# Windowed attention and a gated low-rank feed-forward: the gated factors carried in the block moves, the feed-forward product in two parts, value differences from SBUF, queries normed in place

## The chip, the cores and the metric

One Trainium2 chip, one of its cores. The metric is the device time of one execution in microseconds. Everything is float32.

## The reference, cut to what matters

There are 32 sequences of 512 tokens of 256 features, 16 query heads and 4 key heads of 64 features, a window of 128 tokens, and a feed-forward with 8 gated low-rank parts of rank 16.

```python
x = x + attn(layernorm(x)); x = x + ffn(layernorm(x))

def attn(x, wq, wk, wv, wo, q_norm_w, k_norm_w):
    q, k, v = rmsnorm(x @ wq.T, q_norm_w), rmsnorm(x @ wk.T, k_norm_w), x @ wv.T   # per head
    scores = q k^T / 8, kept where (i >= j) & (i - j < 128)
    return (softmax(scores) @ v) @ wo.T

def ffn(x, weight, gate_w, lora_U, lora_V):
    gate = softmax(x @ gate_w.T)                       # 8 gates
    base = x @ weight.T
    t = einsum('nh,erh->ner', x, lora_U)               # 8 x 16 factors
    lora = einsum('ne,eor,ner->no', gate, lora_V, t)
    return base + lora / 16
```

## The kernel before, in words

The work is cut into 128 tiles of 128 tokens, four to a sequence (`t` = 0 to 3). A tile passes through a pipeline of small steps. `slot(i)` writes out one turn of the pipeline: it names, in order, which step is issued for which tile, so while tile `i` has its inputs transposed (`trx`), tile `i-3` has its scores made (`s_pe`), tile `i-6` its values summed (`y_pe`), tile `i-7` its output product (`o_pe`), tile `i-10` its feed-forward product (`f_pe`), and tile `i-11` is stored. The order within each engine is exactly the order of this list; nothing is reordered later. The first 12 turns are in a table `FIRST`, the last ones in `LAST`, and `slot(i)` runs for i = 12 to 127. `BANK` and `PLACES` fix which of four single PSUM banks (B0 to B3) a product goes to; the scores have two double banks (S0, S1) of their own, each used twice in a turn.

What each step does, with its engine and line:

- TensorE (PE): `kv_pe` L398 and `q_pe` L413 are the key, value and query products (two chunks of 128 features, 512 columns each; a float32 product is two instructions, so four per 512 columns). `s_pe` L529 makes scores for 32 queries of a head pair against 160 keys. `y_pe` L627 multiplies probabilities and values in 16 half-width instructions, then, for `t` > 0, adds a correction in 16 quarter-size ones. `o_pe` L654 is the output product, 16 instructions of 256 columns. `f_pe` L700 multiplies the normed hidden rows by 392 columns at once: 128 of lora_U, 8 of the gate and 256 of the base weight, into one bank `f`. `uT_pe` L731 transposes the gated factors `u`, one instruction of 128 columns. `lora_pe` L738 adds lora onto the base columns that still lie in the bank `f`.
- ScalarE (ACT): copies and squares of k, v and q out of PSUM (L404, L408, L421, L426), `q_eps` L441, the exponentials `exps` L556 (16 per tile, each with an accumulator read), `y_copy` L648, `kT_copy` L511, `hT_copy` L690, `uT_copy` L735, `gexp` L714, and `ln1_neg` L385, which makes minus the row scale for `vdiff`.
- VectorE (DVE): sums of squares (`qsum` L435), the score merge and maximum (`s_merge` L540, `nmaxs` L545), transposes of 32x32 blocks (`tr`, `trk`, `trq`, `trh`, `trx`), `vdiff` L613 and L616 (the difference between a tile's values and the values of the tile before), `o_add`, `gmax`, `gmul` L720, `store` L745.
- GpSimd (POOL): all powers (`pow` L319 for the norms of q and k, and the two layer-norm scales), `kn` and `qn` (keys and queries times their norms), `prob` L568 (exponentials times the reciprocal of their sum), `pick` L599 (masks for the correction in `y_pe`).
- SyncE (SP): DMA issues. A transpose on VectorE only turns 32x32 blocks; the blocks are then sent to their places by `move`, 16 DMAs per tile. What must be transposed is written into one buffer `tr` (`blocks_of(n)`) in pieces: queries (0 to KO), keys (KO to PO), probabilities (PO to HO) and hidden rows (HO on), each of another tile; `move(n)` sends all of them to a buffer `pT` (`moved[n]`), and consumers read their piece. SP also loads x in two layouts and stores the result (`put` L750).

In `vdiff` one operand is the value product in PSUM, the other a tile in SBUF:

```python
nc.vector.scalar_tensor_tensor(
    self.vd[lo], own[lo], self.ln1.rs[lo], old[lo], ALU.mult, ALU.subtract
)
```

Of the kernel before, what the change touches and what calls it, by code (L numbers as in the profile page):

```python
# [8 lines left out]
F32 = mybir.dt.float32  # L9
# [5 lines left out]
P = 128  # L15
D = 256
# [14 lines left out]
def tile_window_attn_lora_ffn(  # L31
# [43 lines left out]

    nc = tc.nc
# [11 lines left out]
    XBUFS = 12  # L88
# [5 lines left out]
    DH = 4  # L94
    KO = NCH * BL
    PO = KO + GP * BL
    HO = PO + NB * 2 * GP * BL
    PIECE = HO + ND * BL
# [9 lines left out]
    for tag, products in {  # L108
        "B0": "tq0 y1 uT",
        "B1": "cqa q0 tq1 y0 o",  # L110
        "B2": "ckv cqb hT tk kv q1",
        "B3": "cf f",
        "S0": "s0 s2",
        "S1": "s1 s3",
    }.items():
        BANK.update(dict.fromkeys(products.split(), tag))
# [3 lines left out]
        ("ckv", 0): "B3",  # L120
        ("cqa", 0): "B2",
        ("cqb", 0): "B0",
        ("q0", 0): "B2",
        ("kv", 0): "B1",
        ("q0", 1): "B3",
        ("q1", 0): "B3",
        ("q0", 2): "B0",
        ("kv", 1): "B0",
        ("cf", 0): "B1",
        ("tq0", 0): "B2",  # L130
        ("tk", 0): "B3",
        ("kv", 2): "B3",
        ("tk", 1): "B0",
        ("tq0", 1): "B3",
        ("tq1", 1): "B3",
        ("q0", 3): "B0",
        ("kv", 3): "B1",
        ("tq0", 2): "B1",
        ("tq1", 2): "B2",
        ("tk", 2): "B1",  # L140
        ("q1", 4): "B0",
        ("q0", 5): "B0",
        ("kv", 5): "B3",
        ("kv", 6): "B0",
        ("y0", 0): "B0",
        ("y1", 0): "B3",
        ("q1", 6): "B3",
        ("y0", 1): "B0",
        ("y1", 1): "B3",
        ("o", 0): "B3",  # L150
        ("o", 1): "B0",
        ("y0", 2): "B3",
        ("y0", 3): "B0",
        ("y1", 3): "B3",
        ("o", 2): "B3",
        ("f", 0): "B0",
        ("y1", 4): "B3",
        ("o", 3): "B0",
        ("uT", 0): "B1",
        ("y1", 5): "B2",  # L160
        ("o", 4): "B3",
        ("y0", -6): "B2",
        ("o", -7): "B0",
        ("y0", -5): "B0",
        ("y1", -5): "B2",
        ("f", -8): "B1",
        ("y0", -4): "B0",
        ("y1", -4): "B2",
        ("o", -4): "B3",
        ("f", -7): "B2",  # L170
        ("y0", -3): "B0",
        ("y1", -3): "B3",
        ("hT", -4): "B0",
        ("y0", -2): "B2",
        ("y1", -2): "B1",
        ("uT", -6): "B1",
        ("o", -2): "B2",
        ("hT", -3): "B0",
        ("f", -5): "B1",
        ("y0", -1): "B2",  # L180
        ("y1", -1): "B3",
        ("uT", -5): "B2",
        ("o", -1): "B0",
        ("f", -4): "B0",
        ("uT", -4): "B1",
        ("uT", -3): "B1",
        ("f", -2): "B0",
        ("uT", -2): "B3",
        ("f", -1): "B2",
        ("uT", -1): "B1",  # L190
    }
    def bank(what, name, i):
# [10 lines left out]
        "qn": 2,  # L203
        "ex": 3,
        "yT": 3,
        "h": 5,
        "hT": 2,
        "u": 2,
        "uT": 2,
        "res": 2,  # L210
        "xT": 3,
        "vd": 7,
# [3 lines left out]
        "kv": 8,  # L216
# [128 lines left out]
    def move(n):  # L345
        if not EARLY - DELTA <= n < N:
            return
        lo = 0 if n + DELTA < N else PO
        hi = PIECE if n >= DH else HO if n >= 0 else PO
        moved[n] = buf("pT", [P, NB, PIECE], str(n))  # L350
        for b in range(NB):
            for c in range(NB):
                nc.sync.dma_start(  # L353
                    moved[n][b * BL : (b + 1) * BL, c, lo:hi],
                    blocks[n][c * BL : (c + 1) * BL, b, lo:hi],
                )

    class Tile:
# [22 lines left out]

        def ln1_neg(self):
            if self.t > 0:
                self.minus_rs = small.tile([P, 1], F32, tag="minus_rs", bufs=8, name=f"minus_rs_{self.n}")
                nc.scalar.activation(self.minus_rs, self.ln1.rs, AF.Copy, scale=-1.0)  # L385
# [70 lines left out]
        def qn(self):  # L456
            self.q_n = buf("qn", [P, QD], self.n)
# [148 lines left out]
        def vdiff(self):  # L606

            if self.t == 0:
                return
            self.vd = buf("vd", [P, KD], self.n)  # L610
            own, old = self.ps["kv"][:, KD:], tiles[self.i - 1].kv[:, KD:]
            lo, hi = slice(0, H), slice(H, P)
            nc.vector.scalar_tensor_tensor(  # L613
                self.vd[lo], own[lo], self.ln1.rs[lo], old[lo], ALU.mult, ALU.subtract
            )
            nc.vector.scalar_tensor_tensor(  # L616
                self.vd[hi], own[hi], self.minus_rs[hi], old[hi], ALU.mult, ALU.add
            )
# [53 lines left out]
        def trh(self):  # L672
            nc.vector.transpose(
                blocks_of(self.i + DH)[:, :, HO:].rearrange("p b (c t) -> p c b t", c=ND),
# [10 lines left out]
        def hT_copy(self):  # L685
# [3 lines left out]
            else:  # L689
                nc.scalar.copy(  # L690
                    self.hT.rearrange("p c (j t) -> p c j t", t=BL),
                    moved[self.i + DH][:, :, HO:].rearrange("p j (c t) -> p c j t", c=ND),
# [4 lines left out]
        def f_pe(self):  # L697
            ps = self.bank("f")
            for c in range(ND):
                nc.tensor.matmul(  # L700
                    ps[:, : UG + D], self.hT[:, c, :], wf_sb[:, c, :],
                    start=(c == 0), stop=(c == ND - 1),
                )

        def gmax(self):
            self.lg = small.tile([P, E], F32, tag="lg", name=f"lg_{self.n}")
            nc.vector.tensor_scalar(self.lg, self.ps["f"][:, ER:UG], self.ln2.rs, None, ALU.mult)
# [8 lines left out]
        def gmul(self):  # L716
# [5 lines left out]
                self.ps["f"][:, :ER].rearrange("p (e r) -> p e r", r=R),  # L722
# [9 lines left out]

        def uT_copy(self):
            self.uT = buf("uT", [P, P], self.n)
            nc.scalar.copy(self.uT, self.ps["uT"][:, :P])  # L735

        def lora_pe(self):
            nc.tensor.matmul(  # L738
                self.ps["f"][:, UG : UG + D], self.uT, wv_sb, start=False, stop=True,
# [3 lines left out]
        def store(self):  # L743
            self.res = buf("res", [P, D], self.n)
            nc.vector.scalar_tensor_tensor(  # L745
                self.res, self.ps["f"][:, UG : UG + D], self.ln2.rs, self.h, ALU.mult, ALU.add
# [21 lines left out]
    def slot(i):  # L768
        at(i).ln1_stats()
        at(i - 1).q_pe(0)  # L770
        at(i - 11).uT_copy()
        at(i).trx()
        at(i - 4).tr(0)
        at(i).ln1_eps()
        at(i - 1).q_copy(1)
        at(i - 4).tr(1)
        at(i).ln1_rs()
        at(i - 11).lora_pe()
        at(i - 1).qsq(1)
        at(i - 4).prob_den(1)  # L780
        at(i - 3).s_pe(0)
        at(i - 8).ln2_stats()
        at(i).ln1_neg()
        at(i - 4).prob(1)
        at(i - 11).store()
        at(i - 1).q_copy(0)
        at(i - 3).s_pe(1)
        at(i - 11).put()
        at(i - 1).qsq(0)
        at(i - 3).s_merge(0)  # L790
        at(i).kv_pe()
        at(i - 3).nmaxs(0)
        at(i - 8).ln2_eps()
        at(i - 1).qsum()
        at(i - 6).pick(1)
        at(i - 10).f_pe()
        at(i - 3).s_merge(1)
        at(i - 3).nmaxs(1)
        at(i).kv_copy()
        at(i - 8).ln2_rs()  # L800
        at(i - 4).tr(2)
        at(i).ksq()
        at(i - 6).y_pe()
        at(i - 1).q_eps()
        at(i - 3).exps(0)
        at(i).ksum()
        at(i - 1).pow()
        at(i).vdiff()
        at(i - 3).exps(1)
        at(i - 4).tr(3)  # L810
        at(i - 10).gmax()
        at(i - 3).s_pe(2)
        at(i - 6).y_copy(0)
        at(i - 3).s_pe(3)
        at(i - 3).prob_den(0)
        at(i - 6).y_copy(1)
        at(i - 3).s_merge(2)
        at(i - 7).o_pe()
        at(i - 10).gexp()
        at(i - 3).nmaxs(2)  # L820
        at(i - 1).kn()
        at(i - 3).s_merge(3)
        at(i - 1).qn()
        at(i - 1).trk()
        at(i - 3).nmaxs(3)
        at(i - 2).kT_copy()
        at(i - 10).gmul()
        at(i - 3).exps(2)
        at(i - 3).prob(0)
        at(i - 1).trq()  # L830
        at(i - 10).uT_pe()
        at(i).q_pe(1)
        at(i - 3).exps(3)
        at(i - 7).o_add()
        at(i - 5).pick(0)
        move(i - 4)
        at(i - 7).trh()
        at(i - 9).hT_copy()
# [5 lines left out]
        ldb:2 ldb:3 mean_kv:0 ldx:0 ln1_stats:0 ldb:0 ldb:1 mean_qa:0 ldx:1 ldx:3 mean_qb:0 sub_kv:0  # L844
        trx:0 ldx:5 ln1_eps:0 trx:1 sub_qa:0 ln1_rs:0 kv_pe:0 kv_copy:0 q_pe.0:0 sub_qb:0 ksq:0
        qsq.0:0 ldwo:0 q_copy.0:0 ln1_stats:1 ksum:0 ldx:4 ldx:2 ln1_eps:1 ln1_stats:2 ln1_stats:4
        q_pe.1:0 kv_pe:1 ln1_eps:2 ln1_rs:1 trx:2 ln1_neg:0 ldb:4 ldx:6 ln1_rs:2 q_pe.1:1 ln1_eps:4
        ln1_stats:3 qsq.1:0 ln1_eps:3 q_copy.1:0 qsum:0 kv_copy:1 vdiff:0 ln1_neg:1 ln1_rs:3 ldb:7
        q_pe.0:1 q_eps:0 ldwf:0 ksq:1 q_copy.1:1 vdiff:1 ldb:5 ln1_rs:4 ln1_stats:5 ldx:8 pow:0
        ldx:9 qsq.1:1 ksum:1 q_pe.0:2 ln1_stats:6 qsq.0:1 ln1_stats:8 kn:0 q_copy.0:1 mean_f:0  # L850
        ln1_eps:5 qsq.0:2 ldb:6 ln1_neg:2 qn:0 tk_pe:0 ln1_neg:4 qsum:1 sub_f:0 trx:3 q_pe.1:2
        q_eps:1 kT_copy:0 q_copy.0:2 pow:1 ln1_stats:9 tq_pe.1:0 ldx:7 ln1_neg:3 kn:1 q_copy.1:2
        kv_pe:2 ln1_eps:8 qsq.1:2 tq_copy.1:0 tq_pe.0:0 ln1_eps:6 kv_copy:2 qn:1 kv_pe:3 ksq:2
        ln1_stats:7 tk_pe:1 tq_copy.0:0 kv_copy:3 ksum:2 s_pe.1:0 qsum:2 s_pe.0:0 q_pe.1:3 ln1_rs:5
        s_merge.1:0 nmaxs.1:0 kT_copy:1 s_merge.0:0 trx:4 ksq:3 q_eps:2 ln1_rs:6 q_pe.0:3 pow:2
        exps.1:0 nmaxs.0:0 exps.0:0 vdiff:2 vdiff:3 ksum:3 qsq.1:3 q_copy.1:3 q_copy.0:3 qsq.0:3
        kn:2 tq_pe.0:1 prob_den.0:0 trx:5 tq_copy.0:1 s_pe.3:0 s_merge.3:0 prob.0:0 nmaxs.3:0 trx:6
# [152 lines left out]
```

## Time and profile before

| | |
|---|---|
| time, median of 3 runs | 2090.65 us (2089.69 to 2091.2) |
| the profiled execution's own time | 2090.21 us |
| its span, first to last instruction | 2088.5 us |
| busy share of the span | PE 99%, DVE 85%, POOL 80%, ACT 73% |
| granted TensorE clock | 1.00 |
| busy share of the 16 DMA engines | about 60% |
| four turns (one sequence) in the middle of the program | 64.24 us, of which PE is busy 64.14, DVE 55.59, POOL 52.16, ACT 47.63 |

In the timeline of one engine a line merges instructions of one kind: when the first starts, how long until the last ends, engine, line, operation, what is written and read, the shape, and how many. PE starts one matmul before the last has ended, so a group's first column minus that of the group before is what the earlier group cost; the second column is longer than that. A weight load (PEld) runs beside the matmul before it.

### The profile page before, as it was taken

Reading aid. Unit: us, or ns where it says so; the run is one execution under the profiler, and the core shown is the slowest. Engines: PE = TensorE matmul, PEld = TensorE weight load, DVE = VectorE, ACT = ScalarE, POOL = GpSimd, SP = SyncE. Lnnn points to the kernel's source line nnn. Section 1 sums busy time; section 2 is a strip of 40 time slices with the busy share of each in tenths; the row PEclk is TensorE's granted clock in tenths of the full one; section 3 lists DMA queues with packets and bytes.
Section 4 is the critical chain, followed back from the end, with each engine's and each line's share of the span. In section 5 each row is a group of like instructions: output and inputs, shape, how many; then the busy total and the mean of one; then the engine's idle time right before and its main releaser. Section 6 shows DMA issues by size and latency. Waiting matters only on the chain.

```text
span 2088.5 us, 43160 instructions
## 1 busy us (share of the span) xinstructions
PE 2071.2 (99%) x12214; PEld 1282.8 (61%) x12214; DVE 1778.1 (85%) x4546; ACT 1530.5 (73%) x6247; POOL 1670.9 (80%) x1291
## 2 busy tenths in 40 slices
PE   8999999999999999999999999999999999999999
PEld 4556666666666666666666666666666666666665
DVE  6988888888888888888888888888898888888884
ACT  6877777777777777777777777777777777777773
POOL 6988778877788788888877887778878888887773
PEclk9999999999999999999999999999999999999999
DMA  5665666566656666665666656665656566656653
GB/s 116 143 154 137 140 144 143 132 140 143 144 133 142 141 140 138 142 144 137 137 142 140 146 134 140 142 146 132 143 136 148 132 143 144 139 135 140 142 130 86
DMA packets 272989, 288.79 MB, mean 138 GB/s; under 512 B 172273, under 2 KB 206705, under 8 KB 272753
## 3 DMA queue, kind: packets, MB, share of 16 engines
q1 hardware_dynamic: 272208, 284.47, 59.6%
q8 instruction: 100, 1.64, 0.4%
q10 hardware_dynamic: 544, 1.57, 0.2%
q14 instruction: 137, 1.11, 0.2%
HBM read 36.71 MB, written 16.78 MB: 26 GB/s over the span
## 4 chain that ended last, share of the span: by engine, by line
PE 89%; ACT 6%; SPq 2%; DVE 1%; DMA 1%; issue 0%; DVEq 0%; ACTq 0%
PE o_ps L654 22%; PE q_ps L413 20%; PE s_ps L529 14%; PE y_ps L627 13%; PE kv_ps L398 11%; PE f_ps L700 6%; ACT ex L556 4%; PE f_ps L738 3%; SPq L353 1%; ACT kv L404 1%; PE uT_ps L731 1%; ACT ksq L408 1%; SPq L238 0%; DVE nmax L545 0%; DMA pT<-tr 0%
## 5 line engine op out<-in xcount | busy, mean ns | idle before, releaser
L556 ACT ACTIVATE ex<-s_ps,nmax 128x128 f32<-128x128 f32 x2048 | 720.5, 387 | 28.5 <-DVE nmax L545 22.3
L319 POOL TENSOR_TENSOR rs<-ss_eps,minus_half 128x20 f32<-128x20 f32 x128 | 453.1, 3539 | 167.1 <-ACT ss_eps L441 165.8
L568 POOL TENSOR_TENSOR ex<-ex,rden 128x1024 f32<-128x1024 f32 x256 | 485.4, 1896 | 96.8 <-DVE rden L564 95.3
L654 PE MATMUL o_ps<-wo_sb,yT 128*128 128x256 f32 x2048 | 475.3, 385 | 0.3 <-ACT yT L648 0.3
L556 ACT ACTIVATION_READ_ACCUMULATOR ex<-s_ps,nmax 128x1 f32 x2048 | 465.9, 228 | 0.0
L413 PE MATMUL q_ps<-wq_sb,xT 128*128 128x512 f32 x1024 | 462.6, 593 | 0.1
L654 PEld LDWEIGHTS o_ps<-wo_sb,yT 128*128 128x128 f32 x2048 | 379.1, 190 | 68.8 <-ACT yT L648 10.6
L545 DVE TENSOR_REDUCE nmax<-s_ps 128x4 f32<-128x512 f32 x512 | 348.6, 681 | 13.0
L529 PE MATMUL s_ps<-kT,pT 64*128 64x160 f32 (+4 forms) x4000 | 335.4, 304 | 3.9 <-ACT ex L556 0.9
L529 PEld LDWEIGHTS s_ps<-kT,pT 64*128 64x128 f32 x4000 | 271.1, 186 | 104.5 <-ACT ex L556 47.0
L599 POOL TENSOR_SCALAR_AFFINE_SELECT other<-pT 64x512 f32<-64x512 f32 x384 | 289.8, 755 | 21.3 <-DMA pT<-tr 5.9
L413 PEld LDWEIGHTS q_ps<-wq_sb,xT 128*128 128x128 f32 x1024 | 184.5, 190 | 192.2 <-issue 173.8
L404 ACT ACTIVATE kv<-kv_ps,ln_rs_a 128x512 f32<-128x512 f32 x128 | 88.3, 690 | 265.0 <-PE kv_ps L398 265.0
L398 PE MATMUL kv_ps<-wkv_sb,xT 128*128 128x512 f32 x512 | 253.5, 617 | 0.6 <-DVE xT L390 0.5
L627 PE MATMUL y_ps<-pT,kv 128*64 128x256 f32 x2048 | 249.3, 385 | 0.0
L458 POOL TENSOR_TENSOR qn<-q,rs 128x1024 f32<-128x1024 f32 x128 | 243.4, 1902 | 0.2
L579 DVE STREAM_TRANSPOSE tr<-ex 128x512 f32<-128x512 f32 (+3 forms) x512 | 240.3, 487 | 2.8 <-DMA pT<-tr 1.1
L421 ACT ACTIVATE q<-q_ps,ln_rs_a 128x512 f32<-128x512 f32 x256 | 176.0, 688 | 51.5 <-PE q_ps L413 50.3
L627 PEld LDWEIGHTS y_ps<-pT,kv 128*64 128x64 f32 x2048 | 135.5, 136 | 125.9 <-ACT ss_eps L441 61.4
L540 DVE COPY_PREDICATED s_ps<-over,s_ps 128x128 f32<-128x128 int32 x512 | 148.4, 290 | 75.4 <-PE s_ps L529 70.8
L700 PE MATMUL f_ps<-wf_sb,hT 128*128 128x392 f32 x512 | 190.1, 494 | 0.1
L426 ACT ACTIVATE qsq<-q_ps,ln_rs_a 128x512 f32<-128x512 f32 x256 | 175.0, 684 | 2.0 <-PE q_ps L413 1.2
(85 smaller groups left out, 2538.3 us busy)
## 6 DMA issues: line engine op xcount, KB each, us to landing
pT<-tr SPq DMA_DIRECT2D x1936, 112.0 KB, 2.3
xb<-in_x_dram SPq DMA_DIRECT2D x256, 64.0 KB, 2.3
x<-in_x_dram SPq DMA_DIRECT2D x128, 128.0 KB, 2.4
out_dram<-res SPq DMA_DIRECT2D x128, 128.0 KB, 2.0
pT<-tr SPq DMA_DIRECT2D x64, 104.0 KB, 2.2
pT<-tr SPq DMA_DIRECT2D x48, 72.0 KB, 2.1
wq_sb<-in_wq_dram ACTq DMA_DIRECT2D x1, 1024.0 KB, 7.4
wo_sb<-in_wo_dram SPq DMA_DIRECT2D x1, 1024.0 KB, 6.5
```

The lines of the kernel that those rows point to most:

```text
L319: nc.gpsimd.tensor_tensor(o, v, minus_half[:, : o.shape[-1]], ALU.pow)
L398: nc.tensor.matmul(ps, self.xT[:, c, :], wkv_sb[:, c, :], start=(c == 0), stop=(c == ND - 1))
L413: nc.tensor.matmul(ps, self.xT[:, c, :], wq_sb[:, c, gp * 512 : (gp + 1) * 512], start=(c == 0), stop=(c == ND - 1),)
L458: nc.gpsimd.tensor_tensor(self.q_n.rearrange("p (g d) -> p g d", d=HD), self.q.rearrange("p g (h d) -> p (g h) d", d=HD), self.rs[:, :NH]. ...
L529: nc.tensor.matmul(ps[:, half, gp, o0:n], qT[rows, gp * P : (gp + 1) * P], self.s.kT[rows, gp, k0 + o0 : k0 + n], start=True, stop=True,)
L545: nc.vector.tensor_reduce(self.nmax[j], ps[:, :, :, :P], AX.X, ALU.max, negate=True)
L556: nc.scalar.activation(self.ex[e][:, c, gp, half], ps[:, gp, half, :P], AF.Exp, bias=self.nmax[j][:, gp, half : half + 1], accum_out=self. ...
L568: nc.gpsimd.tensor_tensor(ex, ex, self.rden[e].rearrange("p c g a -> p (c g a)").unsqueeze(2).to_broadcast([P, 8, P]), ALU.mult,)
L599: nc.gpsimd.affine_select(out=self.other[gp][rows].rearrange("p h (c a q) -> p h c a q", c=2, a=2), in_=fr.rearrange("p h (c a q) -> p h c ...
L627: nc.tensor.matmul(ps[e][half * HD : (half + 1) * HD, gp * 4 * H : (gp + 1) * 4 * H], v[:, v0 : v0 + HD], w.rearrange("p h (c a q) -> p a ...
L654: nc.tensor.matmul(ps[:, :D], self.yT[:, c].rearrange("p e t -> p (e t)"), wo_sb[:, c, :], start=(c == 0), stop=(c == NCH - 1),)
L700: nc.tensor.matmul(ps[:, : UG + D], self.hT[:, c, :], wf_sb[:, c, :], start=(c == 0), stop=(c == ND - 1),)
```

## The change

The gated factors `u` are no longer transposed by TensorE. `tru`, a block transpose on VectorE, writes them into a new piece of the `tr` buffer (UO to PIECE, 32 columns per block), `move` carries them along with the other pieces, and `uT_copy` reads them from `pT` two turns later. The last seven tiles keep the old way.

Since lora comes later now, the feed-forward product is split: `ug_pe` makes the 136 columns of factors and gate for tile `i-10` in a bank `g`; `base_pe` makes the 256 base columns for tile `i-14`, in the same turn in which lora is added and the tile stored.

`vdiff` subtracts the scaled copy of the values in SBUF from that of the tile before, two plain subtractions with both operands in SBUF; `ln1_neg` is gone. `qn` writes the normed queries over the queries. Buffer counts, banks and the whole order (`slot`, `FIRST`, `LAST`, `BANK`, `PLACES`) are set anew. In the new turn TensorE's order is: base(i-14), q(i-1) first half, q(i) second half, scores 2 and 3, factors and gate(i-10), lora(i-14), y(i-6), scores 0 and 1, o(i-7), kv(i).

```diff
-    XBUFS = 12
+    XBUFS = 13
...
+    DU = 7
...
-    PIECE = HO + ND * BL
+    UO = HO + ND * BL
+    PIECE = UO + BL
...
-        "qn": 2,
...
-        "h": 5,
-        "hT": 2,
+        "h": 8,
+        "hT": 5,
         "u": 2,
-        "uT": 2,
+        "uT": 3,
...
-        "vd": 7,
+        "vd": 6,
...
-        "kv": 8,
+        "kv": 7,
...
-        hi = PIECE if n >= DH else HO if n >= 0 else PO
+        hi = PIECE if n >= DU else UO if n >= DH else HO if n >= 0 else PO
...
-        def ln1_neg(self):
-            if self.t > 0:
-                self.minus_rs = small.tile([P, 1], F32, tag="minus_rs", bufs=8, name=f"minus_rs_{self.n}")
-                nc.scalar.activation(self.minus_rs, self.ln1.rs, AF.Copy, scale=-1.0)
...
-            self.q_n = buf("qn", [P, QD], self.n)
+            self.q_n = self.q.rearrange("p g n -> p (g n)")
...
-            own, old = self.ps["kv"][:, KD:], tiles[self.i - 1].kv[:, KD:]
+            own, old = self.kv[:, KD:], tiles[self.i - 1].kv[:, KD:]
...
-            nc.vector.scalar_tensor_tensor(
-                self.vd[lo], own[lo], self.ln1.rs[lo], old[lo], ALU.mult, ALU.subtract
-            )
-            nc.vector.scalar_tensor_tensor(
-                self.vd[hi], own[hi], self.minus_rs[hi], old[hi], ALU.mult, ALU.add
-            )
+            nc.vector.tensor_tensor(self.vd[lo], own[lo], old[lo], ALU.subtract)
+            nc.vector.tensor_tensor(self.vd[hi], old[hi], own[hi], ALU.subtract)
...
-        def f_pe(self):
-            ps = self.bank("f")
+        def f_product(self, what, cols):
+            ps = self.bank(what)
+            n = cols.stop - cols.start
             for c in range(ND):
                 nc.tensor.matmul(
-                    ps[:, : UG + D], self.hT[:, c, :], wf_sb[:, c, :],
+                    ps[:, :n], self.hT[:, c, :], wf_sb[:, c, cols],
                     start=(c == 0), stop=(c == ND - 1),
                 )
+
+        def ug_pe(self):
+            self.f_product("g", slice(0, UG))
+
+        def base_pe(self):
+            self.f_product("f", slice(UG, UG + D))
...
+        def tru(self):
+            nc.vector.transpose(
+                blocks_of(self.i + DU)[:, :, UO:],
+                self.u.rearrange("p e r -> p (e r)").rearrange("p (b d) -> p b d", b=NB),
+            )
+
         def uT_copy(self):
             self.uT = buf("uT", [P, P], self.n)
-            nc.scalar.copy(self.uT, self.ps["uT"][:, :P])
+            if "uT" in self.ps:
+                nc.scalar.copy(self.uT, self.ps["uT"][:, :P])
+            else:
+                nc.scalar.copy(
+                    self.uT.rearrange("p (j t) -> p j t", t=BL), moved[self.i + DU][:, :, UO:]
+                )
```

The new turn, cut to the steps that are new, moved far, or spoken of below:

```diff
     def slot(i):
+        at(i - 14).base_pe()
...
+        at(i - 1).q_pe(0)
...
+        at(i - 1).kv_copy()
...
+        at(i - 8).o_add()
...
+        at(i - 1).vdiff()
+        at(i - 4).prob(0)
+        at(i).q_pe(1)
...
+        at(i - 1).qsum()
...
+        at(i - 10).ug_pe()
...
+        at(i - 14).lora_pe()
...
+        at(i - 6).y_pe()
...
+        at(i).kv_pe()
...
+        move(i - 4)
+        at(i - 3).tr(2)
+        at(i - 12).uT_copy()
+        at(i - 10).tru()
```

## The prediction

> **What bounds the kernel now.** I read the page first (busy shares), then TensorE's timeline over one sequence in the middle, then the chain of work that ended last there, and last the rows of what the change touches.
>
> ```profile
> PE 2071.2 (99%) x12214; PEld 1282.8 (61%) x12214; DVE 1778.1 (85%) x4546; ACT 1530.5 (73%) x6247; POOL 1670.9 (80%) x1291
> ```
>
> TensorE is busy nearly always, but its matmuls overlap, so this alone isn't proof. Its timeline gives one turn from one kv product to the next, and further down two lines of a shorter turn and one with narrow scores:
>
> ```profile
> 1000.55 1.98 PE L398 MATMUL kv_ps<-wkv_sb,xT 128*128 128x512 f32 x4
> 1002.38 1.48 PE L700 MATMUL f_ps<-wf_sb,hT 128*128 128x392 f32 x4
> 1003.78 1.95 PE L627 MATMUL y_ps<-pT,kv 128*64 128x256 f32 x16
> 1005.66 1.09 PE L627 MATMUL y_ps<-other,vd 64*64 64x256 f32 x16
> 1006.69 1.36 PE L529 MATMUL s_ps<-kT,pT 64*128 64x160 f32 x16
> 1007.97 3.72 PE L654 MATMUL o_ps<-wo_sb,yT 128*128 128x256 f32 x16
> 1011.53 0.27 PE L731 MATMUL uT_ps<-ident,u 128*128 128x128 f32 x1
> 1011.64 3.60 PE L413 MATMUL q_ps<-wq_sb,xT 128*128 128x512 f32 x8
> 1015.08 0.59 PE L738 MATMUL f_ps<-wv_sb,uT 128*128 128x256 f32 x2
> 1015.60 1.36 PE L529 MATMUL s_ps<-kT,pT 64*128 64x160 f32 x16
> 1016.89 1.98 PE L398 MATMUL kv_ps<-wkv_sb,xT 128*128 128x512 f32 x4
> ...
> 1022.00 1.73 PE L529 MATMUL s_ps<-kT,pT 64*128 64x160 f32 x16
> ...
> 1031.28 1.11 PE L529 MATMUL s_ps<-kT,pT 64*128 64x32 f32 x16
> 1032.32 1.98 PE L398 MATMUL kv_ps<-wkv_sb,xT 128*128 128x512 f32 x4
> ```
>
> Take differences of the first column. Eight q instructions cost 3.44 us, 0.430 each for 512 columns; the one of 128 columns (uT) costs 0.11. So an instruction costs about its columns times 0.833 ns, plus 2 ns: 0.116 us for 136 columns, 0.216 for 256, 0.329 for 392. Entering a full-size group after scores costs some 0.20 more, leaving one for half-size work 0.09. With these, the turn of 16.34 us is explained without any waiting. The one exception in a sequence is the turn whose y has no correction (`t` = 0): its scores, 1022.00, take 1.66 us to the next group (o at 1023.66) where others take 1.29. The chain of waits shows why:
>
> ```profile
> 1020.07 2.80 ACT ex L556 x16
> 1022.87 0.04 issue
> 1022.91 0.81 PE s_ps L529 x8
> ```
>
> Here 1.66 less 1.29, or 0.37 us, is TensorE waiting for 16 exponentials to free the score banks. So: four turns are 64.24 us, of which 63.87 are TensorE's own work. The kernel is TensorE-bound, with one small stall per sequence, and only less TensorE work, or more stalls, can move it.
>
> **The change, part by part.** The profiled execution took 2090.21 us, its span 2088.5 and 1.7 around it; the median is 2090.65, so sums made on the profile carry over with +0.4.
>
> *uT transpose.* The program has 128 before and 7 after: 121 x 0.109 = 13.2 us off TensorE. In its place come a block transpose on DVE (`tru`; row tr<-ex 128x128, 0.31 us, about 0.23 in a stream), 0.2 us of ACT copy as before but from SBUF, and pieces 928 instead of 896 columns in each of the 16 DMAs of `move`. No new DMA. Issues on SP come every 0.635 us and land after 2.3; 16 take 10.2 us of a turn, and the landing of all is about 12.5 us after the last query transpose. The first readers (`kT_copy`, `hT_copy`) come roughly 13.5 us after it in the new order, so 3.6% more bytes hide. If that cover were gone, kT would wait up to 1 us, and `exps` 0 and 1 behind it, which have over 3 us to spare. `put`, now ahead of `move`, is ready at about 9.5 us of the turn, `move` starts at about 13.8: SP is free between.
>
> *Product in two parts.* Before 4 x 0.329 = 1.316 us a tile; after 4 x 0.116 + 4 x 0.216 = 1.328: +0.012 x 128 = +1.5 us. Unknown is whether a product of 136 columns is as fast as its columns: each has a weight load of 128 columns beside it, and that row lasts 0.19. Ends: 0.116 and 0.190 (+0.30 us a tile). The nearest row is the scores of 32 columns at 1031.28: also one load of 128 columns per step, eight steps in 1.04 us less 0.19 for the change of size, 0.11 each. So loads follow one another at 0.11; I take 0.116. The number of changes between full and half size per turn stays the same (scores twice, y once).
>
> Together -13.2 + 1.5 = -11.7 us, 0.39 per sequence.
>
> *Queries in place.* Same POOL instruction, 1.90 us; below or above that nothing. `q` has two buffers, and `trq` of tile i-2 is long done when tile i's copy is written: 0.
>
> *ln1_neg gone.* 96 x 0.2 us less on ACT, which isn't last: 0.
>
> *Value differences.* Before, 0.46 and 0.49 us with one operand in PSUM. After, 256 elements from two SBUF operands; no row shows that. By the nearest (h<-o_ps,x: 0.41 for 256) 0.3 to 0.4 each, a little less. But here a rule of the Trainium skill speaks against the change: "SBUF — State Buffer", section "SBUF: two separate sides", says that VectorE with two SBUF inputs and GpSimd reading SBUF take a shared port pair in turns, and the later one is blocked for the earlier one's whole instruction. The trace has one instruction on VectorE of a kind which the page also names (one that uses both ports):
>
> ```profile
> 91.05 1.89 POOL L568 TENSOR_TENSOR ex<-ex,rden 128x1024 f32<-128x1024 f32 x1
> 92.90 1.64 POOL L599 TENSOR_SCALAR_AFFINE_SELECT other<-pT 64x512 f32<-64x512 f32 x2
> ```
>
> ```profile
> 92.02 1.08 DVE L295 TENSOR_SCALAR wv_sb<-wv_sb 128x256 f32<-128x256 f32 x1
> ```
>
> It took 1.08 us for 256 elements and ended 0.16 after POOL's product did, at 92.94. So the blocking is real for that kind; by the row alone the differences cost 0.35 each, by the rule 0.35 plus the rest of a POOL instruction. I take the rule.
>
> **Where that lands.** I lay the new turn out by hand from the rows, t = 0 at the base product. TensorE: base 0, q 0.86 and 2.58, scores 2 and 3 at 4.39, factors 5.68, lora 6.25, y 6.77, scores 0 and 1 at 9.67 and 10.32, o 10.96, kv 14.52, end 16.23. The chain that could stop it: q's first half done at 2.8, copied and squared by 4.05, `qsum` to 5.3, merge and maximum of scores 2 and 3 to 7.2, 16 exponentials from 6.3 to 9.2; scores 1 need that bank at 10.15. Slack 0.95 us; in the turn with the short y (1.03 less) about -0.1: a stall of 0.1 against 0.37 before.
>
> `vdiff` stands ahead of `qsum` on DVE; behind it are `ksum`, `ln2_stats`, `trh` (1.2 us together) and then `qsum` at 4.1, so it may end at 2.9 for nothing. It is ready at about 1.0, when the scaled values are copied. POOL then runs the picks (0.75 each), `ln_rs` (0.55) and `prob` (1.90, from about 1.1 to 3.0). A difference that falls behind `prob` ends near 3.7, 0.8 late, within the slack; where the turn before was the one with the masked scores (DVE later by some 0.4, TensorE's turn 0.44 shorter), it can end at 4.2 to 4.4, 1.3 to 1.5 late: 0.35 to 0.6 us of stall, or none if it gets ahead of `ln_rs`. POOL, blocked by 0.3 per difference, has 2 us to spare before `pow`. So per sequence: -0.39, -0.27 to -0.1 by the smaller old stall, 0 to +0.6 by the port. With 30 sequences in the even part, -20 to +4 us. The likeliest is between, the last two about cancelling: -11.7, thus 2079. Start and tail (135 and 58 us, TensorE idle 8 and 5 of them) are ordered anew: +-4 us.
>
> **Rivals.** (1) *The port decides.* If both differences of each of the three tiles fall behind `prob`, the chain to scores 1 is over by 0.6 to 0.8 in two of the four turns: +1.2 per sequence, less 0.39 saved: +0.8 x 30 = +24; in one turn, +6. It turns slower from 0.5 us of new stall per sequence on. I take 2103 for it. For: the rule, and the 1.08 us row. Against: POOL idles between `ln_rs` of the feed-forward and `pow`, and only one `prob` can stand in the way. (2) *Work goes, time stays*: TensorE's saved 0.39 returns as waiting at the score banks, since that chain already sets one turn in four: 2090. For: the 0.37 stall. Against: slack 0.95 in the other three. (3) *Loads bound the narrow product*: +0.30 x 128 - 11.7 = 2117. Against: 0.11 per step in the narrow scores.
>
> **Numbers.** Forecast 2079: 0.57. Rival 1: 0.24. Rival 2: 0.14. Rival 3: 0.05. The range reaches from the full gain, 2069, to rival 1 in one to two turns, 2100. A measurement of this kernel can tell about 0.2% (4 us) from no change. Faster by over 0.2% 0.57, within 0.14, slower 0.29.
>
> **What would show it.** Right: the transpose's row shrinks to 7; the 136-column row advances 0.116 per instruction; four turns near 63.9 us; the differences stretched over 0.35 us where POOL is busy. Wrong: the differences longer than 2 us with TensorE waiting for ACT at the second pair of scores (rival 1); four turns still 64.2 (rival 2); 136 columns at 0.19 (rival 3). A TensorE wait on DMA or on `uT` would be a cause that I don't have.

## The result, and the profile after

The changed kernel takes 2113.45 us, median of 4 runs (2112.68 to 2114.06), the kernel before 2090.32 beside it (4 runs, 2089.69 to 2091.2): a ratio of 1.011, 95% interval 1.0093 to 1.0128. It is slower by 23 us, where 2079 was forecast, in a range from 2069 to 2100.

The page of the changed kernel (its span is 2112.3 us) has nearly the same busy TensorE time as before, though TensorE has less to do:

```profile
PE 2070.5 (98%) x12605; PEld 1336.6 (63%) x12605; DVE 1866.5 (88%) x4667; ACT 1536.9 (73%) x6151; POOL 1677.3 (79%) x1291
```

With the same TensorE work and no stall (the last experiment) the row reads 2055.7. So some 15 us of waiting are counted busy here: a group that waits in its middle counts in part. The row that speaks is DVE, 1778.1 before, 88 us more. The groups by line and shape (busy us in total, then mean ns of one, then idle time before them) say where they are; the first line is the kernel before, the others the changed one:

```profile
L613 DVE SCALAR_TENSOR_TENSOR vd<-kv_ps,ln_rs_a,kv 64x256 f32<-64x256 f32 x96 | 44.5, 463 | 1.2 <-ACT ksq L408 1.2
...
L623 DVE TENSOR_TENSOR vd<-kv,kv 64x256 f32<-64x256 f32 x96 | 139.9, 1457 | 1.3 <-ACT kv L414 1.3
L624 DVE TENSOR_TENSOR vd<-kv,kv 64x256 f32<-64x256 f32 x96 | 41.0, 427 | 1.3
```

The transpose of `u` (L744) is down to 7 instructions, as meant. The first of the two differences, 0.46 us before, now takes 1.46 on the mean (shortest 0.38, longest 2.05); the second, of the same size, 0.43.

One turn shows what follows. First DVE's timeline in the changed kernel (start and duration in us), then POOL's in the same stretch:

```profile
927.97 0.16 DVE L574 RECIPROCAL rden<-den 128x8 f32<-128x8 f32 x1
...
928.34 2.04 DVE L623 TENSOR_TENSOR vd<-kv,kv 64x256 f32<-64x256 f32 x1
930.40 0.42 DVE L624 TENSOR_TENSOR vd<-kv,kv 64x256 f32<-64x256 f32 x1
...
932.08 1.18 DVE L445 TENSOR_REDUCE ss<-qsq 128x16 f32<-128x1024 f32 x1
```

```profile
927.58 0.55 POOL L334 TENSOR_TENSOR ln_rs_a<-ln_v_a,minus_half 128x1 f32<-128x1 f32 x1
928.21 1.90 POOL L578 TENSOR_TENSOR ex<-ex,rden 128x1024 f32<-128x1024 f32 x1
```

`prob` ends at 930.11, the difference at 930.38, 0.27 later. Note the order: DVE's own reciprocal (`prob_den`, ended 928.13) is what lets `prob` start, and `vdiff` stands one short instruction behind it on DVE. In all 58 turns of the program where the difference takes some 2 us, `prob` starts within 0.1 us behind that reciprocal; in 26 of them POOL's own `ln_rs` ends in the same moment, as here. So in two of the three turns of a sequence that have differences, the first one starts 0.13 us after `prob` and waits out almost all of it; in the third it meets a mask (`pick`) and takes 0.62.

Behind the differences DVE still has `ln2_stats`, whose variance ACT needs, and then `qsum`. ACT's timeline (the bracket is the idle time before, and who ended it):

```profile
931.86 0.20 ACT L346 ACTIVATE ln_v_f<-ln_mv_f 128x1 f32<-128x1 f32 x1 [1.65 <-DVE ln_mv_f L341]
...
932.54 0.68 ACT L436 ACTIVATE qsq<-q_ps,ln_rs_a 128x512 f32<-128x512 f32 x1
...
934.28 0.37 ACT L566 ACTIVATE ex<-s_ps,nmax 128x128 f32<-128x128 f32 x1 [0.78 <-DVE nmax L555]
```

ACT stood idle for 1.65 us ahead of `ln_v_f`, while the second half of q, ready in PSUM, waited behind it in ACT's order. TensorE then waits twice:

```profile
932.41 0.59 PE L762 MATMUL f_ps<-wv_sb,uT 128*128 128x256 f32 x2
933.27 1.95 PE L633 MATMUL y_ps<-pT,kv 128*64 128x256 f32 x16 [0.27 <-ACT qsq L436]
...
936.17 0.81 PE L539 MATMUL s_ps<-kT,pT 64*128 64x160 f32 x8
937.24 0.81 PE L539 MATMUL s_ps<-kT,pT 64*128 64x160 f32 x8 [0.25 <-ACT ex L566]
937.98 3.72 PE L660 MATMUL o_ps<-wo_sb,yT 128*128 128x256 f32 x16
...
949.50 0.59 PE L762 MATMUL f_ps<-wv_sb,uT 128*128 128x256 f32 x2
```

From lora to y are 0.86 us, 0.53 where nothing waits (the bank of y held q's second half): 0.33 lost. From the scores to `o` are 1.81 us, 1.29 without a wait: 0.52 lost to the exponentials, though the row marks only 0.25 as idle. From lora to lora this turn takes 17.09 us, 16.23 without waits. Taken the same way, most sequences have one more such turn, with 0.42 lost (the one with the short y), and two with nothing lost. Four turns take 64.88 us against 64.24 before.

### The profile page after: what moved, and what is told of

Same layout as the page of the kernel before. It is cut to its first block, busy times and chain, and to the rows that moved or that the text cites. A ratio compares the mean times of both kernels' runs of the same rounds, so it can differ in the third digit from the quotient of the medians.

```text
span 2112.3 us, 44184 instructions
## 1 busy us (share of the span) xinstructions
PE 2070.5 (98%) x12605; PEld 1336.6 (63%) x12605; DVE 1866.5 (88%) x4667; ACT 1536.9 (73%) x6151; POOL 1677.3 (79%) x1291
## 4 chain that ended last, share of the span: by engine, by line
PE 47%; SPq 24%; DVE 11%; DMA 6%; ACT 6%; issue 3%; POOL 1%; ACTq 0%; DVEq 0%
SPq L368 24%; PE o_ps L660 10%; PE q_ps L423 10%; PE y_ps L633 8%; PE s_ps L539 8%; DMA pT<-tr 6%; PE kv_ps L408 5%; ACT ex L566 5%; DVE nmax L555 3%; PE f_ps L707 3%; PE g_ps L707 2%; DVE tr L483 2%; PE f_ps L762 1%; DVE s_ps L550 1%; DVE tr L477 1%
## 5 line engine op out<-in xcount | busy, mean ns | idle before, releaser
L566 ACT ACTIVATION_READ_ACCUMULATOR ex<-s_ps,nmax 128x1 f32 x2048 | 459.0, 224 | 0.0
L539 PE MATMUL s_ps<-kT,pT 64*128 64x160 f32 (+4 forms) x4000 | 343.4, 305 | 20.7 <-ACT ex L566 17.9
L423 PEld LDWEIGHTS q_ps<-wq_sb,xT 128*128 128x128 f32 x1024 | 193.2, 190 | 192.7 <-issue 155.7
L589 DVE STREAM_TRANSPOSE tr<-ex 128x128 f32<-128x128 f32 (+3 forms) x512 | 240.7, 488 | 17.4 <-POOL ex L578 10.7
L468 POOL TENSOR_TENSOR q<-q,rs 128x1024 f32<-128x1024 f32 x128 | 243.6, 1903 | 0.0
L408 PE MATMUL kv_ps<-wkv_sb,xT 128*128 128x512 f32 x512 | 241.3, 593 | 0.1
L445 DVE TENSOR_REDUCE ss<-qsq 128x16 f32<-128x1024 f32 x128 | 153.4, 1199 | 63.5 <-ACT qsq L436 63.4
L334 POOL TENSOR_TENSOR ln_rs_f<-ln_v_f,minus_half 128x1 f32<-128x1 f32 x128 | 70.4, 551 | 143.1 <-ACT ln_v_f L346 142.3
```

What stands on the lines that cost most here:

```text
L334: nc.gpsimd.tensor_tensor(o, v, minus_half[:, : o.shape[-1]], ALU.pow)
L408: nc.tensor.matmul(ps, self.xT[:, c, :], wkv_sb[:, c, :], start=(c == 0), stop=(c == ND - 1))
L423: nc.tensor.matmul(ps, self.xT[:, c, :], wq_sb[:, c, gp * 512 : (gp + 1) * 512], start=(c == 0), stop=(c == ND - 1),)
L468: nc.gpsimd.tensor_tensor(self.q_n.rearrange("p (g d) -> p g d", d=HD), self.q.rearrange("p g (h d) -> p (g h) d", d=HD), self.rs[:, :NH]. ...
L539: nc.tensor.matmul(ps[:, half, gp, o0:n], qT[rows, gp * P : (gp + 1) * P], self.s.kT[rows, gp, k0 + o0 : k0 + n], start=True, stop=True,)
L566: nc.scalar.activation(self.ex[e][:, c, gp, half], ps[:, gp, half, :P], AF.Exp, bias=self.nmax[j][:, gp, half : half + 1], accum_out=self. ...
```

## The experiments

Each run was timed beside the kernel before; the ratio is to that.

| kernel | us | ratio, 95% interval | four turns, us |
|---|---|---|---|
| changed | 2113.45 | 1.0110 (1.0093 to 1.0128) | 64.88 |
| own values from PSUM again | 2078.17 | 0.9945 (0.9933 to 0.9958) | 63.68 |
| differences on POOL | 2072.63 | 0.9918 (0.9905 to 0.9932) | 63.60 |
| before's instruction, both operands SBUF | 2112.78 | 1.0104 (1.0090 to 1.0118) | 64.87 |
| statistics ahead of the differences | 2111.96 | 1.0106 (1.0093 to 1.0120) | 64.89 |
| differences behind the store | 2143.14 | 1.0254 (1.0240 to 1.0268) | 66.03 |
| differences just ahead of qsum | 2096.02 | 1.0025 (1.0016 to 1.0033) | 64.35 |
| before, SBUF differences beside pow | 2090.93 | 0.9999 (0.9990 to 1.0007) | 64.25 |
| before, SBUF differences beside prob | 2143.73 | 1.0255 (1.0241 to 1.0269) | 66.09 |
| differences beside pow | 2087.24 | 0.9984 (0.9977 to 0.9990) | 64.10 |
| the same, o_add earlier | 2073.11 | 0.9919 (0.9905 to 0.9933) | 63.60 |

My theory from the trace: the SBUF differences are blocked by POOL's product, and the delay reaches TensorE over qsum, maxima and exponentials, and over ACT's order. Rival: the new order, the banks, the split product or the carried factors make the stalls.

**Own values from PSUM again.** The changed kernel, `vdiff` of tiles 12 to 126 in the old form:

```diff
+            if 12 <= self.i <= N - 2:
+                own = self.ps["kv"][:, KD:]
+                nc.vector.scalar_tensor_tensor(
+                    self.vd[lo], own[lo], self.ln1.rs[lo], old[lo], ALU.mult, ALU.subtract
+                )
+                nc.vector.scalar_tensor_tensor(
+                    self.vd[hi], own[hi], self.minus_rs[hi], old[hi], ALU.mult, ALU.add
+                )
+                return
...
         at(i - 3).exps(1)
+        at(i).ln1_neg()
```

> The changed kernel, but the value differences of tiles 12 to 126 read the tile's own values from PSUM again, with the scale (or its negative, made by one 0.2 us copy on ACT) applied in the same instruction, as the kernel before does; nothing else moved. Theory (the shared port): the stretched rows vanish (0.46 to 0.49 us each), TensorE's waits for exponentials at the scores and for the squares at y fall to the kernel before's level or under, four turns go from 64.88 to 63.5 to 63.9 us, and the time is 2075 to 2082 us. Rival (the new order, the banks, the split product or the carried factors make the stalls, and DVE's difference only happens to be long): four turns stay near 64.9 and the time within 5 us of 2113.

```profile
L630 DVE SCALAR_TENSOR_TENSOR vd<-kv_ps,ln_rs_a,kv 64x256 f32<-64x256 f32 x86 | 40.2, 467 | 9.2 <-ACT ksq L423 9.2
```

2078.17 us; the differences take 0.47 and 0.49 at the same place on DVE, beside the same `prob`. TensorE waits for exponentials 1.9 us in the whole program, 17.9 in the changed kernel. All of the loss, and the forecast's own gain, come back with one operand in PSUM (and the instruction that goes with it, which a later run tells apart); the rest of the change is not at fault.

**Differences on POOL.** The same two subtractions issued by POOL, in its idle time between `ln2_rs` and `pow`:

```diff
-        at(i - 1).vdiff()
...
         at(i - 8).ln2_rs()
+        at(i - 1).vdiff()
...
-            nc.vector.tensor_tensor(self.vd[lo], own[lo], old[lo], ALU.subtract)
-            nc.vector.tensor_tensor(self.vd[hi], old[hi], own[hi], ALU.subtract)
+            eng = nc.gpsimd if 11 <= self.i <= N - 2 else nc.vector
+            eng.tensor_tensor(self.vd[lo], own[lo], old[lo], ALU.subtract)
+            eng.tensor_tensor(self.vd[hi], old[hi], own[hi], ALU.subtract)
```

> The changed kernel, but the two value differences run on POOL itself, between the feed-forward's ln_rs and pow, where POOL idles; DVE has none. Theory (the shared port): POOL cannot be in its own way, DVE is freed of 0.8 us as well; each difference costs about 0.6 us on POOL (kn, of the same 256 columns, takes 0.61), pow starts at most 0.3 us later; four turns 63.5 to 63.7, time 2074 to 2080 us. Rival (other parts of the change): within 5 us of 2113. A third way: POOL becomes late for pow and kn, and with them the moved pieces, and TensorE waits for kT: over 2085 us with TensorE waiting on kT.

They take 0.72 and 0.73 us on POOL rather than 0.6, and it fits: 2072.63 us, with the last run below the best of all. Its four turns, 63.60 us, have no stall that the trace shows, so 63.60 is what TensorE's own work takes in the new order.

**The instruction or the operands?** The changed kernel with the old instruction, but both operands in SBUF:

```diff
-            nc.vector.tensor_tensor(self.vd[lo], own[lo], old[lo], ALU.subtract)
-            nc.vector.tensor_tensor(self.vd[hi], old[hi], own[hi], ALU.subtract)
+            nc.vector.scalar_tensor_tensor(
+                self.vd[lo], own[lo], 1.0, old[lo], ALU.mult, ALU.subtract
+            )
+            nc.vector.scalar_tensor_tensor(
+                self.vd[hi], old[hi], 1.0, own[hi], ALU.mult, ALU.subtract
+            )
```

> The changed kernel with the value differences in the kernel before's instruction (scalar_tensor_tensor, here with a factor of 1.0), but with both operands in SBUF. It parts the kind of instruction from the place of its operands. Theory (two SBUF operands take the shared port): the first difference is as long as in the changed kernel (about 1.5 us on the mean, up to 2.05), the time within 4 us of 2113. Rival (the plain difference of two tensors is the form that is blocked, the other is not): rows of 0.46 and 0.49 us, 2078 us.

```profile
L623 DVE SCALAR_TENSOR_TENSOR vd<-kv,kv 64x256 f32<-64x256 f32 x96 | 139.9, 1458 | 1.3 <-ACT kv L414 1.3
```

2112.78 us, and the row is within a nanosecond of the changed kernel's. It is where the operands lie.

**Which of the two paths?** The feed-forward statistics ahead of the differences:

```diff
+        at(i - 8).ln2_stats()
         at(i - 1).vdiff()
...
-        at(i - 8).ln2_stats()
```

> The changed kernel with the statistics of the feed-forward norm put ahead of the value differences on DVE instead of behind them; qsum stays behind the differences. This takes away only the path from the blocked difference over ln2_stats and ln_v_f on ACT to the squares that y waits for (0.3 us in one turn of four). If the two paths add: 30 x 0.3 = 9 us less, 2104 us. If the late qsum, maxima and exponentials bind anyway: the wait only moves from y to the scores, and the time stays at 2109 to 2114 us. Rival (ordering on ACT is the whole cause, not the port): waits at y and at the scores both vanish, about 2080 us.

2111.96 us. The wait at y is gone, and waits for exponentials grew from 17.9 to 24.2 us. The differences moved too: on the mean the first now takes 1.00 us and the second 0.93. In one turn of four POOL now starts its product between the two, and the second is the blocked one (2.08 us). So the blocking itself is not the same as in the changed kernel, and the run is no clean test of the paths. It fits that they don't add (the late maxima bind, and time given back at y is waited at the scores), but doesn't show it.

**A later place on DVE.** The SBUF differences moved behind the store:

```diff
-        at(i - 1).vdiff()
...
+        at(i - 1).vdiff()
         at(i - 3).prob_den(1)
```

> The changed kernel with the same two SBUF differences on DVE, moved behind the store, where DVE idles and no TensorE chain hangs on what follows at once (POOL is then at the end of pow or at kn and qn). Theory (blocking matters only through what stands behind it on DVE): rows may still be stretched to 1 to 2 us, yet four turns are 63.5 to 64.0 us and the time 2075 to 2085 us. Rival (the rest of the change makes the stalls): within 5 us of 2113. If the blocked place only moves the delay to the next maxima or merges: between, 2090 to 2105, with waits at the first pair of scores instead of the second.

A miss: 2143.14 us. In one turn of four `vdiff` meets POOL's `kn` and product of q (the first takes 0.71, the second 2.03 us). Behind it on DVE now stand `gmul` and `o_add`, and TensorE waits for both, as its timeline in this kernel shows:

```profile
937.11 1.98 PE L423 MATMUL q_ps<-wq_sb,xT 128*128 128x512 f32 x4 [0.98 <-DVE u L733]
940.02 1.98 PE L423 MATMUL q_ps<-wq_sb,xT 128*128 128x512 f32 x4 [0.93 <-DVE h L667]
```

The reason is the new banks: q's first half takes the bank of `g`, which `gmul` reads, its second half the bank of `o`, which `o_add` reads. So this place on DVE, which had looked free, was not.

**Just ahead of qsum.**

```diff
-        at(i - 1).vdiff()
...
+        at(i - 1).vdiff()
         at(i - 1).qsum()
```

> The changed kernel with the SBUF differences moved on DVE behind ksum, the feed-forward statistics and trh, just ahead of qsum: some 1.2 us later, when POOL's prob is nearly over, and nothing but qsum and what follows behind it. Theory (what is lost is the rest of prob): the first difference falls from 1.5 us on the mean to 0.4 to 1.0; the wait at y goes; what is left of the delay of qsum is 0.3 to 0.9 us against a slack of about 0.95: 2078 to 2092 us. Rival (the place on DVE, not the port, makes the stalls): as the changed kernel, 2108 to 2114 us. If the feed-forward's ln_rs, which POOL then takes up right behind prob, gets in between: the second difference is blocked as well, and the time is above 2092 us.

2096.02 us, 4 over the expected range. `prob` is nearly over in two turns of three that have differences (0.83 us in one, in most sequences 0.38 in the other), but in the third POOL is late by its masks, `prob` starts at 967.82 just ahead of the difference at 968.05, and that one takes 1.94. That turn is 16.73 us instead of the 15.98 that it has without stall; the other three have none.

**Another neighbour on POOL.** The kernel before, with SBUF differences alone:

```diff
-            own, old = self.ps["kv"][:, KD:], tiles[self.i - 1].kv[:, KD:]
+            own, old = self.kv[:, KD:], tiles[self.i - 1].kv[:, KD:]
...
+            nc.vector.tensor_tensor(self.vd[lo], own[lo], old[lo], ALU.subtract)
+            nc.vector.tensor_tensor(self.vd[hi], old[hi], own[hi], ALU.subtract)
```

> The kernel before with one part of the change alone: the two value differences take both operands from SBUF (tensor_tensor, as in the changed kernel); everything else, the order too, is the kernel before's. There the differences stand right beside POOL's pow, which takes 3.54 us. Theory (the shared port; the stretch is the rest of the POOL instruction, whichever it is): the first difference grows from 0.46 to about 3 to 3.5 us in three turns of four, DVE is late by over 2 us for the merges and for u, TensorE waits for uT and for the exponentials: slower than before, 2100 to 2160 us. Rival (the stretch belongs to the changed kernel's order or banks): rows of 0.4 us, within 3 us of 2090.

My theory failed here in part: 2090.93 us, no difference. DVE's and POOL's timelines in this kernel:

```profile
1004.55 0.40 DVE L613 TENSOR_TENSOR vd<-kv,kv 64x256 f32<-64x256 f32 x1
```

```profile
1004.26 3.54 POOL L319 TENSOR_TENSOR rs<-ss_eps,minus_half 128x20 f32<-128x20 f32 x1 [1.19 <-ACT ss_eps L441]
```

The difference starts 0.29 us into a POOL instruction of 3.54 and isn't blocked at all. So not every POOL instruction blocks. The counterpart moves the same differences, in the same kernel, beside the second `prob`:

```diff
         at(i - 8).ln2_stats()
+        if i > 12:
+            at(i - 1).vdiff()
...
-        at(i).vdiff()
...
+        at(N - 1).vdiff()
         in_order(LAST, N)
```

> The kernel before with SBUF differences, as in the earlier run that cost nothing, but issued one turn later and moved on DVE from beside pow to behind the feed-forward statistics, where POOL is at the second prob (1.90 us). Same kernel, same instruction, only the neighbour on POOL differs. Amended theory: the first difference grows from 0.40 to 1.3 to 2.1 us where it falls behind prob, the merges and maxima of scores 0 and 1 come over 1 us late, and the short turn's wait for exponentials grows from 0.4 to over 1 us: 2095 to 2135 us. Rival (the blocking belongs to the changed kernel): rows of 0.4 us, within 5 us of 2091.

```profile
1006.88 1.82 DVE L613 TENSOR_TENSOR vd<-kv,kv 64x256 f32<-64x256 f32 x1
1008.72 0.87 DVE L614 TENSOR_TENSOR vd<-kv,kv 64x256 f32<-64x256 f32 x1
```

```profile
1006.53 1.90 POOL L568 TENSOR_TENSOR ex<-ex,rden 128x1024 f32<-128x1024 f32 x1 [0.63 <-DVE rden L564]
```

2143.73 us, somewhat more than the range allowed; in two turns of three the second difference is caught by a mask (`pick`) right behind `prob` and takes 0.87, which I had not reckoned with. With nothing of the change but the SBUF operands, the place alone decides between no loss and 53 us. The rows show the blocking (1.82 instead of 0.40); how much of the 53 us an unblocked difference would cost at that place on DVE was not run.

**Beside pow, in the changed kernel.**

```diff
-        at(i - 1).vdiff()
...
         at(i - 3).nmaxs(3)
+        at(i - 1).vdiff()
```

> The changed kernel with the SBUF differences moved on DVE behind the maxima of scores 3 and ahead of tr 0, where POOL runs pow (3.54 us). In the kernel before with SBUF differences (an earlier run) they ran beside pow in 0.40 and 0.42 us, unblocked. Amended theory (POOL's products block, its powers do not): rows of 0.38 to 0.43 us, four turns 63.6 to 63.7 us, 2072 to 2080 us. Rival (any POOL instruction blocks in this kernel, and the earlier run escaped for another reason): rows up to 3.5 us, DVE late for tr, gmax and the merges, above 2110 us.

The rows are as expected, 0.42 and 0.43 us. The time isn't: 2087.24. One turn of four still loses 0.5 us (16.49 instead of 15.98); TensorE's timeline in this kernel (the first two lines are the turn with the short y):

```profile
954.73 1.49 PE L539 MATMUL s_ps<-kT,pT 64*128 64x160 f32 x16
956.15 3.72 PE L660 MATMUL o_ps<-wo_sb,yT 128*128 128x256 f32 x16
...
980.19 1.98 PE L423 MATMUL q_ps<-wq_sb,xT 128*128 128x512 f32 x4 [0.23 <-DVE h L667]
```

q's second half waits for `o_add`, the bank again: some 0.8 us of differences now stand in DVE's stretch ahead of `o_add`. So I put `o_add` ahead of `tr` 3:

```diff
+        at(i - 8).o_add()
         at(i - 4).tr(3)
...
-        at(i - 8).o_add()
```

> The kernel of the run before last (SBUF differences beside pow) with o_add of tile i-8 put ahead of tr 3 and prob_den on DVE, some 0.9 us earlier. There TensorE's second half of q waited 0.5 us in one turn of four for h, the sum that reads the o bank, which q takes over (B1 holds q1, y0 and o). Theory (that wait is all that is left of stall): four turns fall from 64.10 to 63.60 us and the time by about 14 us, to 2070 to 2076 us; the differences stay at 0.42 us each. Rival (DVE is simply over by 0.5 us a sequence in that turn, whatever the order): the wait shows up elsewhere, 2083 to 2090 us.

2073.11 us, four turns 63.60. Both this and the version with POOL beat both kernels.

## Why the prediction was wrong, point by point

- *TensorE's own work.* Right. Own work of four turns is 63.60 us in the new order. Before, it is 64.24 us less the stall, and here I had misread the 0.37 us: scores behind a y without correction take 1.42 us to `o` with nothing waited for (954.73 to 956.15 above), not 1.29. So of the 0.37 stall only 0.24 was waiting, and own work was 64.00. The saving is 0.40 per sequence; I had 0.39, made of the transpose and the split product. Rival 3 (narrow product bound by its loads) is out: 0.30 a tile more would be 1.2 per sequence, and the 136-column instructions of one product start 0.116 apart.
- *The cover of the moved pieces, of `uT_copy`, `tru`, queries in place.* No wait of TensorE on `uT` or on a DMA appears in the even part; the version without stall bears it out. The changed kernel's page gives SyncE's issues 24% of the chain that ended last, but the only thing that the stalled scores at 937.24 wait for is an exponential, and ACT is busy without a gap from 934.28 until then; with the values read from PSUM that share is 2%.
- *Start and tail, +-4.* The span less 30 times four turns is 161.3 us before and 165.9 after, 4.6 more. Some 1.8 of that are seven sequences with up to 0.35 us more, so start and tail stayed within what I allowed.
- *The step that failed: "So per sequence: -0.39, -0.27 to -0.1 by the smaller old stall, 0 to +0.6 by the port ... the last two about cancelling."* The stall went from 0.24 to 1.28 us (0.86 and 0.42 in two turns): +1.04, not about 0. 0.40 saved and 1.04 lost are +0.64 per sequence, times 30 is 19 us, and 4.6 from start, tail and longer sequences make the 23.8 by which the two profiled spans differ. The mechanism, the rule of the Trainium skill that I took ("SBUF — State Buffer", section "SBUF: two separate sides"), was right for the instruction that stood in the way, a product; its size wasn't. Three terms of it were wrong:
  - I let `vdiff` be ready at 1.0 us of the turn and `prob` run from about 1.1 to 3.0, so that a blocked difference ended near 3.7. The scaled values are there at 1.7 and DVE reaches it at 2.2 (928.34 with the base product at 926.16), because `prob_den` and `o_add` stand ahead of it, and `prob_den` is what starts `prob`. So `prob` begins just ahead of the difference, ends at 3.95, and the second difference at 4.66. That is 1.0 later than my figure and 1.76 later than the 2.9 that costs nothing: 0.8 more than the slack of 0.95 covers.
  - I followed only `qsum`. ACT's order carries the same delay from `ln2_stats` to q's squares, and so to y.
  - I counted one turn with 0.35 to 0.6 us. Two turns lose, and the worst 0.86.
- *Rival 1* ("in two of the four turns ... 0.6 to 0.8 ... +24") is what came: two turns, 1.04 in sum. It deserved the forecast. That its +24 is so near the measured 23 is partly luck: it put 1.2 per sequence where 1.04 came, and start, tail and longer sequences made up the rest. I had weighed against it that only one `prob` can stand in the way; one is enough when it always does.
- *Rival 2* is out: where the blocking goes, the saved work shows in the time (2072.63).

## What to carry to other kernels

Before an elementwise step on VectorE gets its second operand from SBUF too, look at what GpSimd runs at that place in the order: read the differences of start times in both timelines, and ask whether an instruction on VectorE itself releases the GpSimd one, since then they may meet every time. That the reciprocal makes them meet is read from the start times; no run moved it. If they meet, keep one operand in PSUM (+23 us became -12 here), give the step to GpSimd (-17), or put it beside a power rather than a product (-3, and -17 when `o_add` was moved as well). A delay on an in-order engine must be followed on every engine that takes something behind it, and through the banks that those readers hold.

## What the runs showed of the hardware that I had not expected

- POOL's products and masks block a two-SBUF-operand difference on DVE: it ends 0.27 us after the product, 0.25 after a mask (product of 1024 columns 1.90 us: difference up to 2.05). POOL's powers don't: 0.40 and 0.42 us inside a power of 3.54 us, in nearly every tile of three kernels. The Trainium skill's section says the lock is held against any GpSimd instruction that reads SBUF; for the powers the measurement decides otherwise. Why they are exempt was not tried. The exemption has one direction: a power that starts while a difference still runs is held up (the feed-forward's `ln_rs` took 0.73 instead of 0.55 us in 29 turns of the kernel before with the differences beside `prob`).
- Two differences in a row are not blocked twice by one product. The second is blocked only where POOL has its next product or mask waiting: 2.03 us behind the product of q, 0.87 behind a mask, 0.42 otherwise.
- POOL is slowed in turn, but little: the product of q took 2.08 instead of 1.90 us where a difference was ahead of it, 0.18 more, as with the power.
